# Attention logits and softmax denominators as extra columns of the large products, in a graph-attention and sliced-attention kernel

## The chip, the cores and the metric

The kernel runs on one core of a Trainium2 chip. The metric is the device time of one execution in microseconds (us). All products are of fp32 operands. Medians may be compared to within some 4 us.

Engine names are those of the profile: PE is TensorE, PEld its weight loads, DVE VectorE, ACT ScalarE, POOL GpSimd.

## The reference, cut to what matters

`x` is `[32, 512, 256]`: 32 batches of 512 tokens. The hidden width is 512.

```python
def _gat(inp, adj_mask, W, a):                 # called unmasked (width 512), then masked (width 256)
    h = jnp.matmul(inp, W)
    f1 = jnp.matmul(h, a[:F_, 0])              # two logits for each token
    f2 = jnp.matmul(h, a[F_:, 0])
    e = jax.nn.leaky_relu(f1[:, :, None] + f2[:, None, :], ALPHA)
    if adj_mask is not None:
        e = jnp.where(adj_mask[None, :, :] > 0, e, NEG_INF)
    att = jax.nn.softmax(e, axis=2)
    return jax.nn.elu(jnp.einsum('bij,bjf->bif', att, h))

# graph part: mlp1, unmasked _gat, mlp2, masked _gat, each with residual
...
# sliced attention: 8 heads of 64 slices, 64 channels
slice_weights = softmax((x_mid @ W_slice + b_slice) / temp)
slice_token = einsum('bhnc,bhng->bhgc', fx_mid, slice_weights) / (slice_norm + 1e-5)
q, k, v = slice_token @ W_q, slice_token @ W_k, slice_token @ W_v
attn = softmax(einsum('bhgc,bhkc->bhgk', q, k) * SCALE)
...
```

## The kernel before

Two generators share the instruction stream. `front(b)` does layer norm, first MLP and unmasked attention; `back(b - 1)` does second MLP, masked attention and sliced attention of the batch before. A loop takes one step (up to the next `yield`) of each in turn.

```python
def logit_columns(srcT, wa, kk):                         # f1 and f2 straight from the input: x (W a)
    pf = sm_tile([P, NT, 2])
    for t in range(NT):
        for k in range(kk):
            nc.tensor.matmul(pf[:, t, :], srcT[:, k, ts(t)], wa[:, k, :], ...)   # two columns wide
    ...

# --- front: unmasked attention
f = logit_columns(o0T, wa1, KH)                          # before the large product h
h = big("h")
for t in range(NT):
    pm = mm_tile([P, HID])
    for k in range(KH):
        nc.tensor.matmul(pm, o0T[:, k, ts(t)], wfc[:, k, :], ...)
    ...                                                  # evicted by DVE or ACT in turn
    if t == 0:   fm = max over tiles of f2
    if t == 1:   transpose of fm, max -> f2m; five small DVE ops and exp -> ex
    if t == 3:   eight transposes of ex, copies -> acb   # A and C of each token, along the free axis
    yield
pT = big("pT")                                           # unnormalised probabilities, transposed
for j in range(NT):                                      # eight DVE operations of 512 columns
    nc.vector.tensor_scalar(pT[:, j, :], acb[:, 1, :], ex[:, 3, j : j + 1], None, op0=OP.mult)
    nc.vector.scalar_tensor_tensor(pT[:, j, :], acb[:, 0, :], ex[:, 2, j : j + 1], pT[:, j, :],
                                   op0=OP.mult, op1=OP.max)
yield
for i in range(NT):                                      # denominators: one column wide
    for j in range(NT):
        nc.tensor.matmul(pd[:, i : i + 1], pT[:, j, ts(i)], ones, ...)
nc.vector.reciprocal(rd, pd)
for i in range(NT):                                      # the product pT h, then double elu
    ...
        nc.tensor.matmul(pm, pT[:, j, ts(i)], h[:, j, :], ...)
    nc.vector.tensor_scalar(u, pm, rd[:, i : i + 1], None, op0=OP.mult)
    elu_elu(u, m)
    ...

# --- back, sliced attention
for p in range(NP):                                      # sums of weights, one row each
    nc.tensor.matmul(pn[:, ts(p)], s1[:, p, D : D + 1], ident, ...)
for p in range(NP):
    ...                                                  # wfx products, then one bias product for each p
    nc.tensor.matmul(pm[:, p, :], bfx[:, ts(p)], nrow[:, ts(p)], start=False, stop=True)
for s in range(2):
    nc.vector.tensor_copy(tokbd[ts(s, C), :, ts(s, G)], pm[ts(s, C), :, ts(s, G)])
nc.tensor.matmul(pq, wq2, tokbd, ...)                    # queries, keys, values
nc.tensor.matmul(pk, wk2, tokbd, ...)
...
```

## Time and profile before

| | before |
|---|---|
| median of the first 3 runs, us | 3814.86 (3810.12 to 3816.15) |
| span of the profiled execution, us | 3797.6 |
| mean period of a batch, us | 116.63 |
| half clock in the trace's clock records, us in all | 359 |

"Half clock" is the time in which the trace's clock records show TensorE's clock granted at half.

I cut a batch's period at starts in TensorE's timeline, and took the mean of 29 middle batches: **S1** from the second MLP's product to the first transposes of `e`; **S2** to the first product with `p2T` (the large product `h` of the front half lies here); **S3** to the transposes of `s1` (the products with `pT` and the masked attention's tail lie here); **S4** to the output product (the sliced attention); **S5** to the next period. Before they take 21.16, 21.03, 46.92, 20.18 and 7.34 us.

The timeline: the columns are start, length, engine, line, operation, output <- inputs, shapes, count, and in brackets the idle time before and its releaser.

```profile
2000.82 0.88 DVE L347 TENSOR_SCALAR pT<-acb,ex 128x512 f32<-128x512 f32 x2 [0.85 <-ACT acb L342]
2001.62 1.40 DVE L350 SCALAR_TENSOR_TENSOR pT<-acb,ex,pT 128x512 f32<-128x512 f32 x2
...
2003.74 1.41 DVE L350 SCALAR_TENSOR_TENSOR pT<-acb,ex,pT 128x512 f32<-128x512 f32 x2
```

All eight operations run, 4.3 us from 2000.82 to 2005.15, while TensorE does the product with `p2T` (1999.95 to 2006.86 in its own timeline). `pT` is whole when TensorE turns to it.

### The profile page before, as it was taken

The numbers are of one execution on the slowest core, as the hardware profiler recorded it, in microseconds if no ns is written. First come the engines' busy times: TensorE is split into PE (matmuls) and PEld (weight loads), VectorE is DVE, ScalarE is ACT, GpSimd is POOL, SyncE is SP. The second block draws the span as 40 slices with busy tenths as digits, with TensorE's granted clock in tenths as the row PEclk, the third lists the DMA queues.
The fourth block names the chain that finished last, engine by engine and source line by source line (L and its number), as shares of the span: only waits on it lengthen the run. The fifth ranks groups of instructions, "written<-read, shape, count | busy, mean of one in ns | idle before, by whom it ended". The sixth has DMA issues, their size and how long they took to land.

```text
span 3797.6 us, 37270 instructions
## 1 busy us (share of the span) xinstructions
PE 3573.3 (94%) x14793; PEld 2310.7 (61%) x14793; DVE 1847.3 (49%) x4213; ACT 1079.6 (28%) x1988; POOL 333.5 (9%) x328
## 2 busy tenths in 40 slices
PE   6999999999999999999999999999999999999997
PEld 3666565666666666566656566666666656665655
DVE  4544445534555444555445554455544455534454
ACT  1322223222223222233222322222322223222232
POOL 0100111000111001110011110011100111001100
PEclk9999999999999999999999999999999999999999
DMA  2000000000000000000000000000000000000000
GB/s 81 6 11 6 12 12 6 11 12 6 12 6 12 12 6 12 11 6 12 6 12 12 6 12 12 6 12 9 9 12 6 12 12 6 12 6 12 6 1 12
DMA packets 39984, 42.02 MB, mean 11 GB/s; under 512 B 3457, under 2 KB 37889, under 8 KB 39810
## 3 DMA queue, kind: packets, MB, share of 16 engines
q1 hardware_dynamic: 37008, 37.50, 3.1%
q8 instruction: 117, 1.92, 0.2%
q10 hardware_dynamic: 2802, 2.14, 0.2%
q14 instruction: 57, 0.47, 0.0%
HBM read 22.85 MB, written 16.78 MB: 10 GB/s over the span
## 4 chain that ended last, share of the span: by engine, by line
PE 81%; DVE 12%; ACT 4%; POOL 1%; issue 1%; DMA 1%; SPq 0%; POOLq 0%; ACTq 0%; DVEq 0%
PE mm L304 12%; PE mm L377 10%; PE mm L634 6%; PE mm L399 6%; PE mm L293 6%; PE mm L472 6%; PE mm L542 5%; PE sm L264 4%; PE mm L410 3%; PE sm L369 3%; PE mm L621 3%; PE mm L567 2%; PE tr L253 2%; PE tr L438 2%; DVE mx L518 1%; DVE o1T L365 1%
## 5 line engine op out<-in xcount | busy, mean ns | idle before, releaser
L377 PE MATMUL mm<-h,pT 128*128 128x512 f32 x1024 | 510.4, 650 | 0.0
L304 PE MATMUL mm<-wfc,o0T 128*128 128x512 f32 x1024 | 495.0, 623 | 0.0
L377 PEld LDWEIGHTS mm<-h,pT 128*128 128x128 f32 x1024 | 205.8, 209 | 230.0 <-issue 230.0
L304 PEld LDWEIGHTS mm<-wfc,o0T 128*128 128x128 f32 x1024 | 189.8, 198 | 180.3 <-issue 180.3
L240 POOL TENSOR_SCALAR rstd<-mv 128x4 f32<-128x4 f32 x64 | 27.8, 435 | 2889.5 <-DVE mv L238 2889.5
L274 ACT ACTIVATE m<-m 128x512 f32<-128x512 f32 x192 | 121.0, 630 | 463.7 <-DVE m L273 463.7
L542 PE MATMUL mm<-xn,w 128*128 128x257 f32 x1024 | 243.1, 380 | 0.0
L511 PE MATMUL mm<-weff,xn2T 128*128 128x512 f32 x512 | 241.6, 595 | 0.0
L634 PE MATMUL mm<-gg,wT 128*128 128x256 f32 x1024 | 239.6, 394 | 0.0
L293 PE MATMUL mm<-xnT,w 128*128 128x512 f32 x512 | 230.3, 593 | 0.6 <-ACT xnT L257 0.6
L399 PE MATMUL mm<-o1T,w 128*128 128x512 f32 x512 | 227.5, 597 | 0.8 <-DVE o1T L365 0.8
L634 PEld LDWEIGHTS mm<-gg,wT 128*128 128x128 f32 x1024 | 207.2, 203 | 33.8
L472 PE MATMUL mm<-h,p2T 128*128 128x256 f32 x1024 | 227.5, 380 | 0.0
L542 PEld LDWEIGHTS mm<-xn,w 128*128 128x128 f32 x1024 | 187.1, 190 | 35.3 <-issue 14.8
L472 PEld LDWEIGHTS mm<-h,p2T 128*128 128x128 f32 x1024 | 192.4, 191 | 25.1 <-ACT p2T L442 0.2
L637 DVE TENSOR_TENSOR y<-mm,x 128x512 f32<-128x512 f32 x64 | 44.2, 691 | 307.2 <-PE mm L634 307.2
L526 POOL TENSOR_TENSOR w<-w,rs 128x512 f32<-128x512 f32 x128 | 155.9, 1218 | 401.0 <-DVE rs L525 359.8
L276 DVE SCALAR_TENSOR_TENSOR u<-m,u 128x512 f32<-128x512 f32 x192 | 135.0, 703 | 84.0 <-ACT m L275 83.9
L399 PEld LDWEIGHTS mm<-o1T,w 128*128 128x128 f32 x512 | 98.1, 192 | 111.4 <-issue 108.6
L453 ACT ACTIVATE e<-e,nmax 128x512 f32<-128x512 f32 x128 | 92.0, 718 | 249.3 <-DVE fm L314 143.7
L402 ACT ACTIVATE o2T<-mm,b 128x512 f32<-128x512 f32 x64 | 44.0, 688 | 403.6 <-PE mm L399 403.6
L446 DVE SCALAR_TENSOR_TENSOR e<-f2b,f,mbias 128x512 f32<-128x512 f32 x128 | 93.0, 748 | 132.1 <-PE tr L438 120.5
(154 smaller groups left out, 5428.9 us busy)
## 6 DMA issues: line engine op xcount, KB each, us to landing
xt<-in_x_dram SPq DMA_DIRECT2D x32, 512.0 KB, 3.9
out_dram<-y SPq DMA_DIRECT2D x32, 512.0 KB, 2.9
w<-in_L_gnn_mlp_w_dram SPq DMA_DIRECT2D x2, 512.0 KB, 7.7
wfc<-in_L_gnn_W_fc_dram ACTq DMA_DIRECT2D x1, 1024.0 KB, 9.5
adjt<-in_adj_dram SPq DMA_DIRECT2D x1, 1024.0 KB, 8.1
wfx<-in_L_ffn_W_fx_dram ACTq DMA_DIRECT2D x1, 512.0 KB, 11.6
wo<-in_L_ffn_W_out_dram ACTq DMA_DIRECT2D x1, 512.0 KB, 3.9
ab<-in_L_gnn_a_fc_dram SPq DMA_DIRECT2D x1, 512.0 KB
```

What stands on the lines that cost most here:

```text
L264: nc.tensor.matmul(pf[:, t, :], srcT[:, k, ts(t)], wa[:, k, :], start=(k == 0), stop=(k == kk - 1))
L274: nc.scalar.activation(m, m, AF.Exp)
L276: nc.vector.scalar_tensor_tensor(t, m, -1.0, t, op0=OP.add, op1=OP.max)
L293: nc.tensor.matmul(pm, w1[:, k, ts(m)], xnT[:, k, :], start=(k == 0), stop=(k == KD - 1))
L304: nc.tensor.matmul(pm, o0T[:, k, ts(t)], wfc[:, k, :], start=(k == 0), stop=(k == KH - 1))
L377: nc.tensor.matmul(pm, pT[:, j, ts(i)], h[:, j, :], start=(j == 0), stop=(j == NT - 1))
L399: nc.tensor.matmul(pm, w2[:, k, ts(m)], o1T[:, k, :], start=(k == 0), stop=(k == KH - 1))
L472: nc.tensor.matmul(pm[:, s, :], pT[:, j, ts(i)], h[:, j, :], start=(j == 0), stop=(j == NT - 1))
L511: nc.tensor.matmul(pm, xnT[:, k, ts(t)], weff[:, k, :], start=(k == 0), stop=(k == KD - 1))
L526: nc.gpsimd.tensor_tensor(w3, w3, rs[:, :, None].to_broadcast([P, HEADS, G]), op=OP.mult)
L542: nc.tensor.matmul(pm, w[:, t, ts(p)], xn[:, t, :], start=(t == 0), stop=(t == NT - 1))
L634: nc.tensor.matmul(po[:, s, :], wT[:, p, ts(t)], gg[:, p, :], start=(p == 0), stop=(p == NP - 1))
```

## The change

Matmuls of one or two columns are to vanish. The logits' weights `W a` become the 257th column of each half of `wfc` and two more columns of `wh`, so that the large products give the logits as well. `h` gets a column of ones in the place of its first logit, so that the product with `pT` gives the denominators. In the sliced attention `W_q W_k^T` is formed once in setup, so that one projection takes the place of two; four bias products become one; the copies onto the block diagonal go to two or three engines. In both attentions `u` is now scaled half by DVE and half by ACT, where DVE had done all of it in the unmasked and ACT all in the masked one. The diff, cut to its core:

```diff
-        f = logit_columns(o0T, wa1, KH)
-        h = big("h")
+        h = big("h", (P, NT, 2, HH + 1))
         for t in range(NT):
-            pm = mm_tile([P, HID])
-            for k in range(KH):
-                nc.tensor.matmul(pm, o0T[:, k, ts(t)], wfc[:, k, :], ...)
+            for s in range(2):
+                pm = mm_tile([P, HH + 1])
+                for k in range(KH):
+                    nc.tensor.matmul(pm, o0T[:, k, ts(t)], wfc[:, k, s, :], ...)
 ...
-            if t == 0: ... if t == 1: ... if t == 3: ...      # max, ex, acb under the product
-            yield
+            yield
+        f1, f2 = h[:, :, 0, HH], h[:, :, 1, HH]
+        ...                                                  # max, f2m, ex: behind the product
+        nc.scalar.activation(ex, ex, AF.Exp)
+        yield
+        nc.vector.memset(f1, 1.0)
+        ...                                                  # transposes of ex, acb
+        yield
 ...
-        for i in range(NT):
-            for j in range(NT):
-                nc.tensor.matmul(pd[:, i : i + 1], pT[:, j, ts(i)], ones, ...)
-            pm = mm_tile([P, HID])
+            pms = [mm_tile([P, HH + 1]), mm_tile([P, HH])]   # 257 and 256 columns
+            nc.vector.reciprocal(rd, pms[0][:, HH : HH + 1])
+            elu_elu(...)                                     # half of the scaling on DVE, half on ACT
 ...
-        f = logit_columns(o2T, wa2, KD)
+                nc.tensor.matmul(pm, o2T[:, k, ts(t)], wh[:, k, :], ...)   # 258 columns
 ...
-            nc.tensor.matmul(pm[:, p, :], bfx[:, ts(p)], nrow[:, ts(p)], start=False, stop=True)
+        nc.tensor.matmul(pm, bfx, nrow, start=False, stop=True)
-        nc.tensor.matmul(pq, wq2, tokbd, ...)
-        nc.tensor.matmul(pk, wk2, tokbd, ...)
+        nc.tensor.matmul(pq, wqk, tok, start=True, stop=True)
```

PSUM is divided anew: five banks for large products instead of four, one for small ones instead of two.

## The prediction

> **What bounds the kernel now.** I read the page first (busy shares, groups of instructions), then the timeline of TensorE over one batch, then the chain of waits and the busy times by stretch for the same batch.
>
> ```profile
> PE 3573.3 (94%) x14793; PEld 2310.7 (61%) x14793; DVE 1847.3 (49%) x4213; ACT 1079.6 (28%) x1988; POOL 333.5 (9%) x328
> ...
> L377 PE MATMUL mm<-h,pT 128*128 128x512 f32 x1024 | 510.4, 650 | 0.0
> L304 PE MATMUL mm<-wfc,o0T 128*128 128x512 f32 x1024 | 495.0, 623 | 0.0
> ...
> L293 PE MATMUL mm<-xnT,w 128*128 128x512 f32 x512 | 230.3, 593 | 0.6 <-ACT xnT L257 0.6
> ```
>
> TensorE is in use nearly all the time, everything else half of it or less. Each fp32 matmul leaves two records (1024 for the 512 matmuls of L377). Three lines have the same 128x512 shape, but the means are 593, 623 and 650 ns: something slows L304 and L377, and it will matter below.
>
> The timeline of TensorE, one batch:
>
> ```profile
> 1883.65 7.07 PE L472 MATMUL mm<-h,p2T 128*128 128x256 f32 x32
> 1890.56 3.63 PE L369 MATMUL sm<-ones,pT 128*128 128x1 f32 x32
> 1894.05 11.38 PE L377 MATMUL mm<-h,pT 128*128 128x512 f32 x22
> ...
> 1934.50 0.48 PE L570 MATMUL mm<-nrow,bfx 1*128 1x128 f32 x2
> ...
> 1939.10 2.08 PE L579 MATMUL mm<-tokbd,wq 128*128 128x512 f32 x2 [0.95 <-DVE tokbd L574]
> 1940.96 1.50 PE L582 MATMUL mm<-tokbd,wk 128*128 128x512 f32 x2
> 1942.30 1.89 PE L591 MATMUL mm<-wvo,tokbd 128*128 128x256 f32 x8
> ...
> 1966.48 1.84 PE L264 MATMUL sm<-wa,o2T 128*128 128x2 f32 x16
> ...
> 1980.34 0.73 PE L264 MATMUL sm<-wa,o0T 128*128 128x2 f32 x6
> ...
> 1981.87 2.96 PE L264 MATMUL sm<-wa,o0T 128*128 128x2 f32 x26
> ```
>
> The next batch's L369 starts at 2006.86, so a period is 116.3 us and 32 of them are 3722 us; the rest is setup, the first front half and the last back half. Start to start, a record of 256 columns takes (1890.56-1883.65)/32 = 0.216 us. A record of **one** column takes (1894.05-1890.56)/32 = 0.109 us: half as much for 1/256 of the columns. That is what the change goes after.
>
> Busy times by stretch (us; PE, PEld, DVE, ACT, POOL with counts, then the granted clock):
>
> ```profile
> 1894.00:1905.50 11.50, 11.43 (x24) 4.72 (x24) 8.43 (x23) 2.70 (x4) 1.27 (x2) 0.85 0.15 46
> 1905.50:1921.20 15.70, 15.00 (x54) 7.94 (x55) 14.54 (x32) 6.38 (x10) 5.24 (x4) 1.00 0.01 2
> ...
> 1930.60:1951.50 20.90, 17.06 (x73) 11.15 (x73) 5.64 (x16) 4.96 (x10) 0.11 (x1) 0.85 0.00 1
> ```
>
> Three regimes: most of a batch is bound by TensorE; from 1905 to 1921 VectorE is as full (14.54 of 15.70), and the chain of waits runs through DVE there; from 1930.6 to 1951.5 one batch's slice attention runs alone, a serial chain of small matmuls and evictions with TensorE waiting.
>
> [...] clock 0.85 over the 11.50 us behind the one-column burst is 1.7 us lost[...]; L377 x22 took 11.38 where 22 x 0.43 is 9.5. So the near-empty matmuls also slow what follows. From the means: L377 (650-592) x 1024 = 59 us in all, L304 behind the logits (623-592) x 1024 = 32 us, 592 being the median of L377. [...]
>
> **The change, part by part (us per batch).**
>
> *Unmasked logits* (L264 on o0T) go: 6 + 26 records, 0.59 + 2.82 start to start = 3.4. The product with wfc becomes 64 records of 257 columns for 32 of 512. L542 already streams 257 columns, half of them from odd offsets, at 380 ns each, as L472's 256 (380): no penalty for the odd width. 64 x 0.2165 = 13.9 against 32 x 0.43 = 13.8: +0.1. The slowed clock behind them goes too: 32/32 = 1.0. **Saved 4.2**; VectorE is busy 7 of 19 us there and holds nothing.
>
> *Masked logits* (L264 on o2T): 16 records, 1.7; two more columns on 16 records cost 0.03. **Saved 1.6.**
>
> *Denominators* (L369): 32 records, 3.5, and the clock dip behind, 1.8: 5.3 of TensorE time freed. But not all of it counts. The maximum and the exponentials of the logits lay under the product h; now they start after it. In the other batch half, the p2T product (6.9 us) and eight transposes cover: eviction, max, transpose, max, five small DVE operations, exp (some 2.6 us by their rows), transposes 0.9, copies 0.9, then pT's eight DVE operations 4.3 = 8.7, plus whatever VectorE does for x1 in between (1 to 3). So TensorE may stand 1 to 3 us before pT, and VectorE is full afterwards. From the end of h to the last softmax sum VectorE is busy 34.8 of 44.1 us (1999.1 to 2043.2). After: +1.1 for the exponentials' part moved in, +1.0 for half of x1's scaling moved from ACT (2 x 0.48, the 257-column row L548), +0.5 for three more reciprocals, -1.0 for half of u's scaling moved to ACT (4 x (0.74-0.48)): 36.4. With 5 to 6 us of waits that stay (max, exp, rstd), it ends after 42. **Saved 2.6**, not 5.3.
>
> *Slice attention*: four one-row transposes (8 records) become one; the wait for the last s1 and its copies by ACT takes their place: 0.2. Four bias products at 0.41 become one of 512 columns, 0.86, and the interleaving ends: 1.2. The two diagonal copies run on DVE and ACT at once: 0.43 for 0.86: 0.4. Queries and keys took 1.9 (full clock) to 3.2 (half); the merged one takes 0.43 + latency, but the value product now waits for two POOL copies into tokbd. My estimate for those is 0.8 (a POOL memset of 512 columns took 529 ns, so 0.3 each, plus handover): 1.1 to 2.4, taken as 1.5. Sum 3.3; **I take 3.0**, since the clock may dip elsewhere.
>
> Total 4.2 + 1.6 + 2.6 + 3.0 = 11.4; x 32 = 365. Setup: one product and two transposes more, but the wait for DMA (26 us) rules there: +3. 3815 - 365 + 3 = **3453**, put as 3455.
>
> **Rivals.** *A: the freed TensorE time all comes back*, pT in time because the scheduler runs partial sums of several banks ahead (it does so in L542: records of four banks before the last w). For it: five banks, TensorE at 94%. Against: VectorE at 14.54 of 15.70. Then the third term is 5.3: about 3365. *B: a wait takes the place of the denominators*: pT later by the whole chain (8.7 + 3 against 8), a TensorE gap of 4 us, and a new clock dip behind it. The third term falls to 0 or below: 3540 to 3570. For it: pT was finished just in time before (L369 waited 0 in steady state). *C: VectorE or ScalarE becomes the bound for the whole batch*: VectorE totals 57 of 116 us and changes by about 1, ScalarE 34: against it. *D: POOL in the slice chain costs more than estimated*: 1 us more is 32 us.
>
> **Range and chances.** Terms one and two are arithmetic on measured spacing: 5.8 x 32 = 186 us, nearly sure. Third term -0.5 to 5, fourth 2 to 4. 80%: 3385 to 3550. Within 2% means under 2.4 us saved per batch, which needs terms three and four both strongly negative: 2%. Slower: 1%.
>
> **What would show it.** Right: no records with 1 or 2 columns; the 257-column products of h at 380 ns and 0.216 spacing; TensorE records down to about 14793 - 2560 + 2048 - (7 + 6 + 2) x 32; the half clock behind h gone; period near 105 us; VectorE over 90% busy for some 18 us of it. Wrong: a TensorE gap at the first pT product over 3 us or a half clock behind it; 257-column records slower than 400 ns; the value product waiting over 1 us on POOL; VectorE idle in its dense stretch while TensorE is full (then A).

## The result and the profile after

The kernel after takes **3568.9 us** (median of 4; 3567.24 to 3571.1) against 3813.07 (4 runs) for the kernel before in the same rounds. Its ratio is 0.9367, 95% interval 0.9348 to 0.9386. It is faster, as predicted, but by 244 us rather than 360: 114 us above the predicted 3455 and 19 us above the upper end of the range.

From the page of the kernel after (busy times, then the costliest groups):

```profile
PE 3210.7 (90%) x13805; PEld 2382.9 (67%) x13805; DVE 1848.0 (52%) x4375; ACT 1120.2 (31%) x2182; POOL 336.8 (9%) x393
...
L383 PE MATMUL mm<-h,pT 128*128 128x257 f32 (+1 forms) x2048 | 568.4, 428 | 130.6 <-DVE pT L363 130.6
...
L317 PE MATMUL mm<-wfc,o0T 128*128 128x257 f32 x2048 | 464.7, 379 | 0.0
```

The 257-column product with `wfc` costs 379 ns a record, as assumed, and waits 0.0 us. But the product with `pT`, which waited 0.0 us before, now waits 130.6 us in all for `pT` (4.1 a batch), and its mean of 428 ns is longer than 379: it also runs at half clock in part (the granted clock was 0.50 from 1996.40 to 1998.60 us, where four of its records took 2.08 us).

The timeline of TensorE, one batch of the kernel after, around that product:

```profile
1982.87 3.62 PE L480 MATMUL mm<-h,p2T 128*128 128x256 f32 x16
1986.32 0.27 PE L330 MATMUL sm<-ident,fm 128*128 128x128 f32 x1
1986.43 3.62 PE L480 MATMUL mm<-h,p2T 128*128 128x256 f32 x16
1989.88 1.03 PE L352 MATMUL tr<-ident,ex 128*128 128x128 f32 x8
1994.03 1.14 PE L383 MATMUL mm<-h,pT 128*128 128x257 f32 x4 [3.11 <-DVE pT L363]
1996.45 2.08 PE L383 MATMUL mm<-h,pT 128*128 128x257 f32 x4 [1.29 <-DVE pT L363]
1998.83 2.08 PE L383 MATMUL mm<-h,pT 128*128 128x257 f32 x4 [0.30 <-DVE pT L363]
```

Two things are to be seen. First, the chain from the last product of `h` to `pT` passes TensorE twice, for the transpose of the maximum (L330) and for those of `ex` (L352), and each stands in line behind 16 records of the other half's product. Second, TensorE then waits 3.11 us, and the next groups of four records come at the spacing at which `pT` comes, 2.42 and 2.38 us; four records at full clock take 1.14.

The same stretch on DVE:

```profile
1991.78 0.48 DVE L360 TENSOR_SCALAR pT<-acb,ex 128x512 f32<-128x512 f32 x1
...
1993.25 0.72 DVE L363 SCALAR_TENSOR_TENSOR pT<-acb,ex,pT 128x512 f32<-128x512 f32 x1
...
1995.05 0.68 DVE L488 TENSOR_TENSOR u<-u,r 128x512 f32<-128x512 f32 x1
...
1996.31 0.68 DVE L489 SCALAR_TENSOR_TENSOR x<-u,xt 128x512 f32<-128x512 f32 x1
...
2000.48 1.38 DVE L262 TENSOR_SCALAR xn<-x,mv,rstd 128x256 f32<-128x256 f32 x4 [1.24 <-POOL rstd L260]
2001.78 0.74 DVE L363 SCALAR_TENSOR_TENSOR pT<-acb,ex,pT 128x512 f32<-128x512 f32 x1
```

The eight operations that took 4.3 us in one piece now stretch from 1991.78 to 2002.52, 10.7 us: they come later, and between them stand the residual of the masked attention (L488, L489) and the layer norm (L262, and the statistics in the lines left out).

The sliced attention of the kernel after, which answers to the lines from 1934.50 on in the prediction:

```profile
1927.05 1.12 PE L580 MATMUL mm<-nrow,bfx 4*128 4x512 f32 x2
1929.14 0.70 PE L592 MATMUL mm<-tok,wqk 128*128 128x256 f32 x2 [0.96 <-ACT tok L584]
1929.67 2.84 PE L600 MATMUL mm<-wvo,tokbd 128*128 128x256 f32 x8
...
1937.40 3.68 PE L630 MATMUL mm<-vo,attT 128*128 128x256 f32 x8 [0.78 <-DVE attT L623]
```

One bias product, one projection, and the value product (L600) follows it. This view names no wait; the view of line L600 shows that its weight loads wait 7.7 us in all for POOL's copies into `tokbd`, 0.24 a batch, so these are nearly in time. L630's eight records take 3.68 us, where 1.99 is measured below at full clock: the granted clock was 0.54 from 1937.40 to 1941.10 us.

By stretches the change saved 1.75 us in S1, 4.42 in S2, and 2.71 in S4 and S5 together, and **lost 1.59 in S3**. In this account 0.98 us of transposes (of `ex` and of the maximum), which went from S2 to S3, is taken out of both. The sum, 7.29 us, times 32 is 233. The medians differ by 244: the profiled execution of the kernel before, with a span of 3797.6 us, was some 15 us below its median, that of the kernel after (3569.3) was not.

The question is therefore S3: 2.6 us a batch were to be gained and 1.6 were lost.

### The profile page after: what moved, and what is told of

Read it like the earlier page. It is cut to its first block, busy times and chain, and to the rows that moved or that the text cites. A ratio compares the mean times of both kernels' runs of the same rounds, so it can differ in the third digit from the quotient of the medians.

```text
span 3569.3 us, 36002 instructions
## 1 busy us (share of the span) xinstructions
PE 3210.7 (90%) x13805; PEld 2382.9 (67%) x13805; DVE 1848.0 (52%) x4375; ACT 1120.2 (31%) x2182; POOL 336.8 (9%) x393
## 4 chain that ended last, share of the span: by engine, by line
PE 75%; DVE 17%; ACT 4%; POOL 2%; issue 2%; DMA 1%; ACTq 0%; DVEq 0%; SPq 0%; POOLq 0%
PE mm L317 12%; PE mm L383 11%; PE mm L643 7%; PE mm L407 6%; PE mm L305 6%; PE mm L518 6%; PE mm L630 3%; PE mm L480 3%; PE mm L416 3%; PE mm L549 3%; DVE pT L363 2%; PE mm L576 2%; PE mm L600 2%; DVE u L288 2%; PE tr L446 2%
## 5 line engine op out<-in xcount | busy, mean ns | idle before, releaser
L383 PE MATMUL mm<-h,pT 128*128 128x257 f32 (+1 forms) x2048 | 568.4, 428 | 130.6 <-DVE pT L363 130.6
L383 PEld LDWEIGHTS mm<-h,pT 128*128 128x128 f32 x2048 | 416.5, 213 | 257.2 <-DVE pT L363 186.2
L317 PE MATMUL mm<-wfc,o0T 128*128 128x257 f32 x2048 | 464.7, 379 | 0.0
L317 PEld LDWEIGHTS mm<-wfc,o0T 128*128 128x128 f32 x2048 | 377.4, 189 | 50.5 <-issue 0.5
L643 PE MATMUL mm<-gg,wT 128*128 128x256 f32 x1024 | 255.9, 413 | 0.0
L643 PEld LDWEIGHTS mm<-gg,wT 128*128 128x128 f32 x1024 | 219.9, 215 | 38.8
L321 DVE COPY h<-mm 128x257 f32<-128x257 f32 x128 | 54.5, 426 | 268.8 <-PE mm L317 268.8
L533 POOL TENSOR_TENSOR w<-w,rs 128x512 f32<-128x512 f32 x128 | 134.1, 1048 | 455.7 <-DVE rs L532 452.5
L529 ACT ACTIVATE w<-w 128x512 f32<-128x512 f32 x128 | 80.7, 630 | 285.2 <-DVE w L526 285.2
L454 DVE SCALAR_TENSOR_TENSOR e<-f2b,h,mbias 128x512 f32<-128x512 f32 x128 | 93.1, 748 | 141.1 <-PE tr L446 93.9
## 6 DMA issues: line engine op xcount, KB each, us to landing
wfx<-in_L_ffn_W_fx_dram ACTq DMA_DIRECT2D x1, 512.0 KB, 11.8
```

Of the source, the lines that this page charges most:

```text
L317: nc.tensor.matmul(pm, o0T[:, k, ts(t)], wfc[:, k, s, :], start=(k == 0), stop=(k == KH - 1))
L383: nc.tensor.matmul(pm, pT[:, j, ts(i)], h[:, j, s, : HH + 1 - s], start=(j == 0), stop=(j == NT - 1),)
L533: nc.gpsimd.tensor_tensor(w3, w3, rs[:, :, None].to_broadcast([P, HEADS, G]), op=OP.mult)
L643: nc.tensor.matmul(po[:, s, :], wT[:, p, ts(t)], gg[:, p, :], start=(p == 0), stop=(p == NP - 1))
```

## The experiments

**Theory L**: the logits come too late. They come with the end of `h`, so the chain to `pT` starts when the other half's work fills both TensorE and DVE; the two engines then take turns where they overlapped. **Theory C**: the clock. The wait itself costs little, and the half clock behind it costs the rest. The expectations also name **theory V**: VectorE's total work sets S3, whenever the logits come. A third possibility is that only the order in the program matters, since `pT` now comes two steps later than it could and loses its turns on DVE. The runs below are in the order in which they tell these apart. Each starts from the kernel after, unless another is named. All outputs are right.

### Early logits by narrow products again

The logits' old products of two columns come back ahead of `h`, with the chain under `h` as before; the denominators stay a column.

```diff
+        pf = sm_tile([P, NT, 2])
+        for t in range(NT):
+            for k in range(KH):
+                nc.tensor.matmul(pf[:, t, :], o0T[:, k, ts(t)], wfc[:, k, :, HH], ...)
+        f = small.tile([P, NT, 2], F32, name="f")
+        nc.vector.tensor_copy(f, pf)
+        ...                        # max at t == 0, ex at t == 1, ones and acb at t == 3, as before
```

> The changed kernel, but the unmasked logits are again a product of two columns ahead of the large one, so that their exponentials and pT lie under it as before; the rest of the change stays. Theory L (the logits come too late, pT waits behind other VectorE work): the stretch from the first p2T product to the first transpose of s1 falls from 49.5 us to 43 or less, the stretch of the large product grows by 3.4 to 4.5 us; net 2 to 3 us per batch gained, about 3490. Theory V (VectorE's total work sets that stretch): it stays at 48 to 49, and the kernel is slower by the narrow product, about 3690.

Measured: 3670.15 us, ratio 0.9631 (0.9617 to 0.9646), so 101 us slower than the kernel after. The total missed the expectation by far, in an informative way. S3 fell from 49.49 to 44.35 us, about what theory L expects. But S2 rose from 15.63 to 21.87, which takes back all of that and more. TensorE's timeline shows why:

```profile
1908.05 2.96 PE L315 MATMUL sm<-wfc,o0T 128*128 128x2 f32 x26
1910.87 4.97 PE L326 MATMUL mm<-wfc,o0T 128*128 128x257 f32 x14
```

The 26 narrow records take 2.8 us to the next start, and the 14 wide ones behind them take 4.97 us where an estimated 14 x 0.217 + 0.16 = 3.2 would do at full clock (spacing 0.217 us, and 0.379 us for one record, from the kernel after). So S2 grew by 6.24 us, 0.98 of it transposes, where the narrow records take 3.4 start to start (0.59 + 2.82). S4 grew as well, by 2.13 us (19.12 for 16.99), with 8.3 us of half clock a batch there for 5.0; that is two thirds of the 101 us, and no run shows whether the narrow products cause it. Here the early logits don't pay as long as they bring such products with them.

### Early logits without narrow products

Both logits become columns of the **first half** of `wfc` (258 columns against 256), and the halves become the outer loop. When the first half of `h` is done, the logits are there, and the chain runs under the second half.

```diff
-    wfc = const.tile([P, KH, 2, HH + 1], F32, name="wfc")
+    wfc = const.tile([P, KH, 2, HH + 2], F32, name="wfc")
-        for t in range(NT):
-            for s in range(2):
+        for q in range(4):
+            s = q // 2
+            w_s = HH + 2 - 2 * s
+            for t in (2 * (q % 2), 2 * (q % 2) + 1):
...
+            if q == 1: ...         # max of f2
+            if q == 2: ...         # transpose, max, ex
+            if q == 3: ...         # ones, transposes of ex, acb
```

> The changed kernel with both logit columns in the first half of the large product (258 and 256 columns) and the halves as the outer loop, so that all logits exist when half of the product is still to come; no matmul more than in the changed kernel. Theory L: the stretch from p2T to s1 falls from 49.5 to 43 us, the stretch before grows by 1 (the broadcast transposes move into it), about 5 us per batch gained, 3390 to 3430. Theory V: stays near 3570.

Measured: **3458.96 us**, ratio 0.9079 (0.9066 to 0.9093): 110 us faster than the kernel after, less than the 140 or more that I expected. S3 is 44.26 us. DVE's timeline has `pT` nearly in one piece again, 4.7 us:

```profile
1924.26 0.88 DVE L361 TENSOR_SCALAR pT<-acb,ex 128x512 f32<-128x512 f32 x2 [1.12 <-ACT acb L356]
1925.06 1.41 DVE L364 SCALAR_TENSOR_TENSOR pT<-acb,ex,pT 128x512 f32<-128x512 f32 x2
...
1928.23 0.74 DVE L364 SCALAR_TENSOR_TENSOR pT<-acb,ex,pT 128x512 f32<-128x512 f32 x1
```

### The same halves, chain late

This is the control: layout and loop of the run before, but the chain stands behind the whole loop, as in the kernel after, with the two hand-overs that it brings there. Nothing else differs.

```diff
-            if q == 1: ... if q == 2: ... if q == 3: ...
             yield
+        ...                        # max, transpose, ex
+        yield
+        ...                        # ones, transposes of ex, acb
+        yield
```

> The kernel of e4_halves, but with the max, exponentials and broadcast put behind the whole product as in the changed kernel: the same matmuls in the same loop order, only the chain later. Theory L: the whole gain of e4_halves goes, 3555 to 3580, pT spread over 10 us again. If the gain came from the loop order or the evictions: near 3459.

Measured: 3567.3 us, ratio 0.9369 (0.9355 to 0.9383): the time of the kernel after, and its S3 (49.45). Columns 258 and 256 and the loop's order are worth nothing by themselves; the place of the chain, with its two hand-overs, is worth 108 us. (By their ratios to the kernel before it is 110.) That is theory L, shown by two kernels that differ in nothing else. How much of it the hand-overs make is seen below.

The new division of PSUM was not tried by itself, but it is not the cause of the loss in S3: with early logits S3 is 44.04 us with the old division (the denominators alone, below) and 44.26 with the new.

The stretches of busy times (length; then PE, PEld, DVE, ACT, POOL busy with counts; granted clock; DMA share; GB/s), S3 of a batch of the kernel before:

```profile
2000.00:2046.90 46.90, 45.37 (x187) 29.37 (x186) 34.88 (x81) 15.93 (x27) 10.30 (x9) 0.96 0.04 12
```

Of the kernel after:

```profile
1982.90:2032.30 49.40, 43.78 (x195) 33.30 (x193) 37.60 (x97) 17.01 (x30) 9.56 (x9) 0.93 0.04 11
```

And S3 with the halves and the early chain:

```profile
1923.40:1967.60 44.20, 40.01 (x187) 30.77 (x185) 36.09 (x86) 16.90 (x29) 9.71 (x9) 1.00 0.04 12
```

DVE is busy 37.60 of 49.40 us, so 11.8 us of S3 pass without it; with the early chain 8.1. TensorE is busy 43.78 of 49.40, part of it at half clock (mean granted clock 0.93). Neither engine is full in the kernel after: each waits for the other in turn (TensorE 130.6 us in all for `pT`). Theory V falls here: from the late to the early chain S3 loses 5.2 us, and DVE's busy time in it 1.5.

### Useless products in the gap before pT

Three products that nobody reads fill the 3.11 us wait. If the clock is what costs, the time falls; if TensorE is paced by `pT`, it does not.

```diff
             nc.scalar.copy(acb[:, s, :], pt)
+        pz = sm_tile([P, N])
+        for _ in range(3):
+            nc.tensor.matmul(pz, ident, o0T[:, 0, :], start=True, stop=True)
         yield
```

> The changed kernel with three useless 128x512 products per batch (never read) behind the broadcast transposes, where TensorE waits for pT: 2.6 us of work in a gap of 3.1. Theory C (the gap makes the clock fall to half, and the half clock costs more than the gap): the half clock behind the gap goes or shrinks, 1.5 to 3 us per batch gained, 3475 to 3520. If the gap alone counts: no change, 3565 to 3580.

Measured: 3566.04 us, ratio 0.9365 (0.9349 to 0.9381): no difference from the kernel after. The filling did what it was to do: the half clock in the trace fell from 473 to 252 us in all. TensorE's timeline:

```profile
1985.76 2.74 PE L358 MATMUL sm<-o0T,ident 128*128 128x512 f32 x6
1989.04 1.14 PE L386 MATMUL mm<-h,pT 128*128 128x257 f32 x4 [0.54 <-DVE pT L366]
1991.46 1.13 PE L386 MATMUL mm<-h,pT 128*128 128x257 f32 x4 [1.29 <-DVE pT L366]
1993.84 1.14 PE L386 MATMUL mm<-h,pT 128*128 128x257 f32 x4 [1.24 <-DVE pT L366]
```

The groups run at full clock (1.13 instead of 2.08 us) and still start 2.42 and 2.38 us apart, to the digit as in the kernel after. What the clock gave back, the wait for `pT` took. Theory C falls for S3.

### pT first in program order

Two hand-overs go, so that the chain and `pT` stand ahead of the other half's next steps and win their turns on DVE.

```diff
         nc.scalar.activation(ex, ex, AF.Exp)
-        yield
 ...
             nc.scalar.copy(acb[:, s, :], pt)
-        yield
```

> The changed kernel with two hand-over points between the batch halves taken out, so that the exponentials, the broadcast and pT stand ahead of the second x1 chunk and its layer norm in program order; no instruction is added or removed. Theory L in its form 'pT loses its turn on VectorE': pT's eight operations take 5 to 6 us instead of 10.7, TensorE's waits before the first pT products (4.7 us) fall under 2, total 3490 to 3530. Theory V: the x1 chain is delayed by the same amount and the total stays within 3550 to 3590.

Measured: 3516.6 us, ratio 0.9235 (0.9222 to 0.9249). It hit what was expected and gains 52 us, half of what the early chain gives. TensorE waits less for `pT`:

```profile
1965.45 9.79 PE L381 MATMUL mm<-h,pT 128*128 128x257 f32 x44 [1.38 <-DVE pT L361]
```

`pT` takes 5.3 us (1963.65 to 1968.96), and these records then run without a wait (the view ended at 1975; there are 48 of them, over 10.7 us). But S3 still takes 47.88 us: the turns that `pT` won, the residual and the layer norm of the masked half lost; in DVE's timeline their next operations start from 1967.8 on. Order shifts the queue; it doesn't make the logits earlier.

### The third hand-over gone too

On top of that, the `yield` behind the last part of `h` goes, so that the chain follows it at once.

```diff
-            yield
+            if t < NT - 1:
+                yield
```

> The kernel of e2_pT_first with the third hand-over gone too: max, exponentials, broadcast and pT stand ahead of the whole masked product in program order, so their transposes don't queue behind its matmuls. If what is left of the loss (47.9 against 44.3 us in that stretch) is this queueing: 45 to 46.5, 3440 to 3490. If TensorE then lacks work to cover the chain, since x1 comes later: 3510 to 3560.

Measured: 3540.99 us (3527.88 to 3548.09, wider than any other), ratio 0.9288 (0.9265 to 0.9311): slower than with two gone, faster than with none, and inside the range expected for the case that x1 comes later. `pT` is now whole 8.7 us behind the end of `h`, for 19.7 in the kernel after, and its products wait 1.0 us a batch; yet S3 is 47.70. Part of the product with `p2T` now runs behind the products with `pT`, so what was won on one half the other half lost. The program order with the shortest S3 still leaves it 3.4 us above that of the early chain, 2.5 when the 0.98 of transposes is taken out.

### Denominators alone, on the kernel before

Only the column of ones and the product in halves, with half of the unmasked `u`'s scaling on ACT, are put into the kernel before; logits stay early and narrow. This measures the step that the prediction priced at 2.6 us.

```diff
-        h = big("h")
+        h = work.tile([P, NT, 2, HH + 1], F32, tag="big", name="h", bufs=6)
+        nc.vector.memset(h[:, :, 0, HH], 1.0)
...
-                nc.tensor.matmul(pd[:, i : i + 1], pT[:, j, ts(i)], ones, ...)
+            pms = [mm_tile([P, HH + 1]), mm_tile([P, HH])]
+            nc.vector.reciprocal(rd, pms[0][:, HH : HH + 1])
```

> The kernel before with one part of the change: the denominators as a column of ones beside h (pT's product in halves of 257 and 256 columns), the logits still early and narrow. The third term of the prediction on its own. If it was right for logits that are early, and only their lateness was missed: 2.6 us per batch in the stretch from p2T to s1, 3725 to 3750. If all of the freed TensorE time counts (5.3 us): about 3640. If the denominators bring nothing even so: 3795 to 3815.

Measured: 3678.04 us, ratio 0.9663 (0.9647 to 0.968), 132 us below before: more than half as much again as I expected. S3 fell by 2.88 us (46.92 to 44.04). The other part is 1.12 us in S4 and S5, where I had expected nothing; half clock fell from 359 to 204 us in all, and in S4 and S5 by 2.5 us a batch, which at half speed is an estimated 1.2 us lost. So the predicted 2.6 was nearly right for the denominators by themselves.

### The old sliced attention

The sliced attention of the kernel before is put back: two projections, four bias products, copies by DVE.

```diff
-        nc.tensor.matmul(pm, bfx, nrow, start=False, stop=True)
+            nc.tensor.matmul(pm[:, p, :], bfx[:, ts(p)], nrow[:, ts(p)], start=False, stop=True)
-        nc.tensor.matmul(pq, wqk, tok, start=True, stop=True)
+        nc.tensor.matmul(pq, wq2, tokbd, start=True, stop=True)
+        nc.tensor.matmul(pk, wk2, tokbd, start=True, stop=True)
...
```

> The changed kernel with the slice attention of before (four bias products, queries and keys apart, one-row transposes). The fourth term of the prediction, 3.0 us per batch: 3569 + 96 = 3665. By the stretches of the two traces (27.5 before, 24.8 after, from the s1 transposes to the second MLP) 2.7: 3655. If the new wait for the POOL copies ate it: 3580 to 3600.

Measured: 3649.51 us, ratio 0.9585 (0.9571 to 0.9599). The part is worth 81 us, 2.5 a batch, where 3.0 was predicted; S4 is 2.78 us longer.

### The old masked logits

```diff
-            pm = mm_tile([P, D + 2])
+        pf = sm_tile([P, NT, 2])
+                nc.tensor.matmul(pf[:, t, :], o2T[:, k, ts(t)], wh[:, k, D:], ...)
+            pm = mm_tile([P, D])
...
```

> The changed kernel with the masked logits again as a product of two columns. The second term of the prediction, 1.6 us per batch: 3569 + 51 = 3620. With a clock dip behind the narrow burst up to 3670, as e1_early_logits has shown for the other logits.

Measured: 3626.12 us, ratio 0.9523 (0.9507 to 0.9539). The part is worth 57 us, 1.8 a batch; 1.6 was predicted. S1 returns to 21.17. No half clock came behind this burst of 16 narrow records: S1 has none in any of the 29 batches.

### Useless products in the sliced attention

In the sliced attention TensorE itself is next on the path after each wait (1.85 and 0.78 us, for `attbd` and `attT`). On top of the early chain with halves, useless products fill two of its waits, so theory C gets its second chance.

```diff
+    def idle(src, n):
+        k, w = src.shape
+        for _ in range(n):
+            pz = mm_tile([P, w])
+            nc.tensor.matmul(pz, ident[:k, :], src, start=True, stop=True)
...
+        idle(vo[:, 2:4, :].rearrange("p a b -> p (a b)"), 2)          # while DVE and ACT make the softmax
         amax = small.tile([P, NP], F32, name="amax")
...
+        idle(attbd[:, 0:3, :].rearrange("p a b -> p (a b)"), 1)       # while DVE copies attT
         attT = work.tile([P, NP, P], F32, name="attT", bufs=1)
```

> The kernel of e4_halves with useless products in the two waits of the slice attention: two of 512 columns behind the scores (a wait of 1.85 us) and one of 384 behind the transposes of the attention (0.78 us). Here TensorE itself is next on the path, unlike in e3_fill. Theory C, for this stretch: the half clock behind it (value-attention product 3.8 for 2.0 us, output product 8.4 for 7.1) shrinks, 1 to 3 us per batch gained, 3365 to 3430. If the clock is worth nothing here either: 3459 within 10.

Measured: **3377.25 us** (3373.57 to 3379.82), ratio 0.8869 (0.8856 to 0.8882): 82 us faster than without the filling, and the fastest version. TensorE's timeline without the filling:

```profile
1981.38 3.78 PE L631 MATMUL mm<-vo,attT 128*128 128x256 f32 x8 [0.78 <-DVE attT L624]
1984.95 8.39 PE L644 MATMUL mm<-gg,wT 128*128 128x256 f32 x32
```

And with it:

```profile
1937.61 1.98 PE L406 MATMUL mm<-vo,ident 128*128 128x512 f32 x4
...
1940.12 0.81 PE L406 MATMUL mm<-attbd,ident 128*128 128x384 f32 x2
1941.13 1.99 PE L640 MATMUL mm<-vo,attT 128*128 128x256 f32 x8 [0.21 <-DVE attT L633]
1942.96 7.07 PE L653 MATMUL mm<-gg,wT 128*128 128x256 f32 x32
```

The same eight records take 1.99 instead of 3.78 us, the 32 of the output product 7.07 instead of 8.39. S4 and S5 fall by 1.5 and 1.05 us; half clock in all falls from 274 to 88 us.

### The scaling of u on ACT alone

On top of that, both halves of `u` in the unmasked attention are scaled by ACT, to see whether DVE's load sets what is left of S3.

```diff
-        nc.vector.tensor_scalar(u[:, cols0], v0, rd0, None, op0=OP.mult)
+        nc.scalar.activation(u[:, cols0], v0, AF.Copy, scale=rd0)      # unmasked attention only
```

> The kernel of e5_halves_fill with both halves of the scaling of u in the unmasked attention on ACT: 4 x 0.48 us per batch less on VectorE, as much more on ACT. If VectorE's total work sets the stretch from p2T to s1 (44.3 us): 1 to 2 us per batch gained, 3310 to 3350. If the chain behind each u sets it (two halves in series on ACT): 3375 to 3420.

Measured: 3385.81 us, ratio 0.8893 (0.8879 to 0.8906): no gain. S3 did shrink, from 44.25 to 43.36, but S4 grew from 16.14 to 17.28 with half clock up from 88 to 181 us. So DVE's load sets part of S3, but the time was given back in the next stretch. No instruction of S4 differs between the two kernels; what raised the half clock I can't take apart with these runs.

### All runs side by side

Stretches are means of 29 batches, in us; "half clock" is the sum over the trace.

| kernel | median us | S1 | S2 | S3 | S4 | S5 | half clock |
|---|---|---|---|---|---|---|---|
| before | 3813 | 21.16 | 21.03 | 46.92 | 20.18 | 7.34 | 359 |
| after | 3569 | 19.41 | 15.63 | 49.49 | 16.99 | 7.82 | 473 |
| early, narrow logits | 3670 | 19.41 | 21.87 | 44.35 | 19.12 | 7.84 | 521 |
| halves, early chain | 3459 | 19.41 | 16.61 | 44.26 | 17.64 | 7.96 | 274 |
| halves, late chain | 3567 | 19.41 | 15.62 | 49.45 | 16.79 | 7.94 | 470 |
| gap before pT filled | 3566 | 19.41 | 15.63 | 49.48 | 17.12 | 7.59 | 252 |
| pT first | 3517 | 19.41 | 15.63 | 47.88 | 17.57 | 7.25 | 269 |
| one step | 3541 | 19.41 | 15.63 | 47.70 | 18.42 | 7.41 | 282 |
| before + denominators | 3678 | 21.16 | 21.04 | 44.04 | 19.31 | 7.09 | 204 |
| old sliced attention | 3650 | 19.41 | 15.63 | 49.81 | 19.77 | 7.41 | 458 |
| old masked logits | 3626 | 21.17 | 15.63 | 50.20 | 16.54 | 7.58 | 473 |
| halves, slices filled | 3377 | 19.41 | 16.61 | 44.25 | 16.14 | 6.91 | 88 |
| the same, scaling on ACT | 3386 | 19.41 | 16.61 | 43.36 | 17.28 | 6.91 | 181 |

## Why the prediction was wrong

**Bound and kind of saving: right.** The narrow records were the cost to go after. TensorE's records are 13805; 13801 was the prediction's sum. The 257-column records take 379 ns at 0.217 us spacing, 380 and 0.216 were assumed. None of the feared penalties of odd widths came.

**Unmasked logits, "Saved 4.2": right in S2**, 4.42 measured. The slowed clock in this term is right too: before, S2 takes 20.05 us in batches without half clock and 21.74 or 23.39 in others, 21.03 in the mean, so 1.0 on average. The early narrow logits confirm that the slowed clock belonged in that term: with the halves and the early chain S2 is 16.61, with narrow products 21.87, a difference of 5.26 us for 3.4 us of matmuls.

**Masked logits, "Saved 1.6": right**, 1.75 in S1 and 57 us (1.8 a batch) by experiment.

**Slice attention, "I take 3.0": nearly right**, 2.71 in S4 and S5 and 81 us (2.5 a batch) by experiment. Rival D falls: the value product's weight loads wait 0.24 us a batch for POOL's copies, not over 1.

**Denominators, "Saved 2.6, not 5.3": this is the step that failed.** Measured were 1.6 us lost in S3, a miss of 4.2 a batch or 134 us, more than the whole miss of 114. Two assumptions carried it.

The first was the chain: 8.7 us from the end of `h` to the whole of `pT`, "plus whatever VectorE does for x1 in between (1 to 3)", so that "TensorE may stand 1 to 3 us before pT". In the kernel after `pT` is whole 19.7 us behind the end of `h` (1982.87 to 2002.52 above; before it was 6.1). The operations that make `pT` begin 8.9 us behind it, since the chain's transposes queue on TensorE, and then take 10.7 us where 4.3 and 1 to 3 were reckoned. The wait before the first product is 3.11 us, just over the range, but the next two groups wait again: 4.7 in this batch.

The second was that "VectorE is full afterwards", with "5 to 6 us of waits that stay". In the stretch that the prediction summed, from the end of `h` to the last softmax sum, DVE is busy 35.4 of 44.5 us in the kernel after (mean of the same 29 batches). So the sum of DVE's work, 36.4, was only 1 us too high; the waits were 9.0, hardly less than the 9.6 before, when a full TensorE explained them. With the early chain the same stretch takes 41.2 us, 35.3 busy and 5.9 of waits: what I had described comes true when the logits are early. With late ones maximum, exponentials, `pT` and products alternate between TensorE and DVE, each queueing behind the other half's work, and a sum of busy time doesn't bound that. S3 as a whole shows the same: DVE stands for 11.8 us of it, for 12.0 before (46.90 - 34.88).

Two slips in that working are small beside this. The view has 34.5 us of DVE from 1999.1 to 2043.2 where the prediction has 34.8; and 36.4 with 5 to 6 of waits ends at 41.4 to 42.4, 1.7 to 2.7 us before 44.1, so that 2.6 was taken from the upper end.

The step has two parts, and the experiments separate them. The denominators by themselves save 2.88 us in S3. The late logits cost 4.2: S3 is 49.45 with the late and 44.26 with the early chain, less 0.98 of transposes that move between S2 and S3. The balance, 1.3 lost, agrees with the 1.6 measured to within 0.3. About half of the late chain's cost is a matter of turns: without the two hand-overs 52 of the 108 us come back.

**Rival B was what happened**: "a wait takes the place of the denominators", third term "to 0 or below: 3540 to 3570"; 3569 was measured. I had named its signs (a gap over 3 us, half clock behind it) and gave it too little weight, since the sum of DVE's work seemed to bound S3 from below. Part of its wording doesn't hold, however: the half clock behind the gap costs nothing in S3, because with it gone the time is the same (S3 49.48 us for 49.49). Rival A falls with the wait. Rival C as stated, an engine that becomes the bound for the whole batch, falls too: DVE is at 52%.

With the chain early and without narrow products, the kernel takes 3459 us, 4 us from the prediction. That is partly luck: its terms are 4.4, 1.75, 2.7 and only 1.9.

**Left open.** The denominators alone gained 1.1 us a batch in S4 and S5, and ACT's scaling lost 1.1 in S4; both go with a changed amount of half clock. What decides where it falls from batch to batch I didn't settle. The runs show half clock in three places: behind TensorE's wait of 3.11 us for `pT` in the kernel after (granted clock 0.50); in some batches behind bursts of 26 to 32 narrow records, with no gap (14 records took 4.97 us where an estimated 3.2 would do; behind 16 narrow records none came); and in the sliced attention, where the waits are of 0.78 to 1.85 us (with the halves and the early chain eight records took 3.78 us instead of 1.99). Transposes and narrow products lie between these last waits, and no run shows which of them counts. Nor is it settled what bounds the rest of S3 at 44 us.

## What to carry to other kernels

When a small result is folded into a large product, ask not only what its own instructions cost but when it was ready and who waits for it: order the product's columns so that the small result comes out of the first part. Price a stretch in which two engines hand work to each other along its chain, with its queueing, and not by the fuller engine's sum. If TensorE itself is next on the path after a wait, try useless products in the wait: here, in waits of 1.85 and 0.78 us, they gave 82 us. Where DVE set its pace, in the wait of 3.11 us, they gave nothing (3566 us for 3569), though half clock fell from 473 to 252 us there as well.
